# A state-space layer, a quantised feed-forward, attention and a latent layer in one kernel: where extractions, additions, broadcasts and PSUM readers stand in the scan loop

## The chip, the cores and the metric

One core of a Trainium2 chip. The kernel's work is spread over the core's engines: TensorE (PE, with weight loads as PEld) multiplies matrices into PSUM, VectorE (DVE), ScalarE (ACT) and GpSimd (POOL) work on tiles of 128 partitions, and SyncE (SP) issues most of the DMAs. Each engine runs its own queue in order and waits on semaphores for the others. The metric is the time of one execution on the device, in microseconds (us), as the median of three runs.

## The reference, cut to what matters

```python
x = x + _layernorm(_L0_attn_ref(_layernorm(x)))   # state-space layer (below)
x = x + _layernorm(_L0_ffn_ref(_layernorm(x)))    # 4-bit weights, unpacked from int32 words
x = x + _layernorm(_L1_attn_ref(_layernorm(x)))   # attention within each token
x = x + _layernorm(_L1_ffn_ref(_layernorm(x)))    # latent and shared feed-forward

# state-space layer: proj = h @ W_in.T; x, gate = halves; x = silu(conv(x))
ts, Bm, Cm = rms(ssm[..., :32]), rms(ssm[..., 32:48]), rms(ssm[..., 48:64])   # ssm = x @ W_x.T
dt = softplus(ts @ W_dt.T + b_dt)
state = state * exp(dt * A) + (dt * x) * B        # over 512 tokens, 1024 channels, 16 states
y = sum_n(state * C) + x * D;  out = (y * silu(gate)) @ W_out.T

# 4-bit weights: q = words[k // 8] >> (k % 8 * 4) & 15;  w = q * s - (z + 1) * s
```

x is 2 x 512 x 512 (batch, token, feature) in float32. The work of this case lies in the state-space layer and in the unpacking of the 4-bit weights, which runs beside it.

## The kernel before

The two batch halves (b = 0, 1) of 512 tokens are worked one after the other. A first part prepares half 0: norm, input projection, convolution, SiLU, the 64 ranks (32 for dt, 16 for B, 16 for C), their norm (`ranks_norm`, line 476) and their transposition (`ranks_out`, line 507), which writes the B and C rows to DRAM (`scr`) and loads them back broadcast to all 128 partitions (`states`, line 515): eight pairs of 512 KB tiles B and C, one pair for every two states.

**The scan loop** (line 1021) then takes 128 steps: 2 halves x 8 channel tiles x 8 pairs of states (`gi`). Of a step s:

- `exps` (ScalarE) makes the decays exp(dt x A) into one of two PSUM buffers,
- `times_B` (VectorE, L976) multiplies dt x u, which lies in PSUM, by the broadcast B into a `bx` tile, one of six,
- `scan` (VectorE, L980) runs the recurrence over 1024 elements, in place,
- `times_C` (GpSimd, L986) multiplies by C, in place,
- `sums` (TensorE, L999) adds the two states into the PSUM tile `y`; at the start of a channel tile a diagonal matmul adds x x D. `fin` (VectorE, L1005) multiplies y into the gate two steps into the next channel tile.

All other work is fitted around these by hand. `stream()` (line 919) is a generator of TensorE work in a fixed order: gate projections of half 0, transposed norms and x projections of half 1, its ranks and gates, the output projection of half 0, and the first tiles of its feed-forward. In each step it is drawn on until a budget of 3.5 us is used. Its results go to two shared PSUM banks, handed out in turn: a tile may take a bank when the one before the last has been released. Whoever reads a bank is a *job*, started with `spawn(generator, lag)`: `tick()` counts half steps in `now[0]` and runs each job that is due; a job's `yield n` puts its next part n half steps on. A step calls `tick()` (odd count, right behind the last scan), then `times_B(s + 1)`, `tick()` (even count), then `scan(s)`, `exps(s + 2)` and `times_C(s)`. `pin()` fixes the order of TensorE, ScalarE, VectorE and GpSimd as traced; SyncE's order is left to the scheduler, which keeps to priorities.

Jobs that this case speaks of: `gate_job` (three ScalarE instructions, and two half steps later a GpSimd product, L652), `x_job` (ScalarE, three convolution instructions on VectorE, L457, ScalarE, a GpSimd product, L703), `dt_job` (softplus on ScalarE between two table loads), `out_job` with `add_normed` and `norm_one` (layer norm and addition to x, L819), `ffn_up_job` (the product of gate and up, L898), and `words_job`. The last starts `gw.steps()` every four half steps: an extraction of four bits of each word on VectorE (`nibble`, L224), a conversion on ScalarE, two GpSimd products with zeros and scales (L278, L279) and a GpSimd DMA to DRAM. It begins with `gw.move` (line 253), which loads the remaining words, scales and zeros into other tiles, since those of the first part are given up; the first of them is needed by the extraction behind scan 3 (counted from 0).

After the loop TensorE finishes the feed-forward tiles that the stream has left, then runs the output projection of half 1 (L1080) and the down projection of half 0 (L1102), while VectorE and GpSimd unpack the down weights (`once`, line 291). The rest of the model follows and is not touched.

Of the kernel before, what the change touches and what calls it, by code (L numbers as in the profile page):

```python
# [18 lines left out]
P = 128  # L19
# [10 lines left out]
N_ST = 16  # L30
# [26 lines left out]
def tile_sandwich(  # L57
# [96 lines left out]
    def xs(b):  # L154
        return x[b * TB : (b + 1) * TB]
# [17 lines left out]
    def normed_T(b, dst, bank, xnew, name, **kw):  # L173
        norm_tiles(b, range(TB), dst, bank, xnew, name, **kw)

    wgu_d = dram.tile([P, 2, KH, INTER], F32, tag="wgu", name="wgu_d")
# [47 lines left out]
    class GateUpWords:  # L226
# [39 lines left out]
        def steps(self, eng=nc.gpsimd):  # L266
            n0, n1, qw, z, s, q_, w_, j = self.todo.pop(0)
            n, nm = n1 - n0, f"gu{n0}_{j}"
            q = q_(nm)
            nibble(q[:, :n], qw[:, :n], j)  # L270
            yield 2
            w = w_(nm)
            if eng is nc.vector:
                eng.tensor_sub(w[:, :n], q[:, :n], z[:, :n])
            else:
                nc.scalar.copy(w[:, :n], q[:, :n])
                yield 2
                eng.tensor_sub(w[:, :n], w[:, :n], z[:, :n])  # L278
            nc.gpsimd.tensor_mul(w[:, :n], w[:, :n], s[:, :n])  # L279
            hp_ = KH * RG  # L280
            rows = slice(j % 2 * hp_, (j % 2 + 1) * hp_)
            nc.gpsimd.dma_start(
                out=wgu_d[rows, :, j // 2, n0:n1].rearrange("r a n -> (r a) n"), in_=w[:, :n]
            )
            yield 2
# [118 lines left out]
    with ExitStack() as mamba:  # L404
# [71 lines left out]
        def ranks_norm(b, ps):  # L476

            sq = jrow(f"sq{b}")[:, : TB * N_ROW].rearrange("p (i r n) -> p i r n", i=TB, n=N_ST)
            nc.scalar.activation(sq.rearrange("p i r n -> p i (r n)"), ps, AF.Square)
            yield 2  # L480
            ss = stat.tile([P, TB, N_ROW // N_ST], F32, tag="ss", name=f"ss{b}")
            nc.vector.tensor_reduce(ss, sq, AX.X, ALU.add)

            nc.vector.tensor_add(ss[:, :, 1], ss[:, :, 0], ss[:, :, 1])
            nc.vector.tensor_scalar(ss[:, :, 1], ss[:, :, 1], 0.5, None, ALU.mult)
            r = stat.tile([P, TB, 3], F32, tag="rr", name=f"rr{b}")
            nc.vector.tensor_scalar(r, ss[:, :, 1:], 1.0 / N_ST, 1e-6, ALU.mult, ALU.add)
            yield 1
            nc.gpsimd.tensor_tensor(r, r, mhalf3, ALU.pow)
            yield 3  # L490
            nb = jrow(f"nb{b}")[:, : TB * N_ROW].rearrange("p (i r) -> p i r", i=TB)
            nc.vector.tensor_mul(
                nb[:, :, :R_DT], ps[:, :, :R_DT], r[:, :, 0:1].to_broadcast([P, TB, R_DT])
            )
            nc.vector.tensor_mul(
                nb[:, :, R_DT:].rearrange("p i (r n) -> p i r n", n=N_ST),
                ps[:, :, R_DT:].rearrange("p i (r n) -> p i r n", n=N_ST),
                r[:, :, 1:3].unsqueeze(3).to_broadcast([P, TB, 2, N_ST]),
            )
            st["nb", b] = nb  # L500
# [116 lines left out]
        with ExitStack() as p2:  # L617
# [11 lines left out]
                das.append(da)  # L629


            jobs, now = [], [0]

            def spawn(gen, lag=0):
                jobs.append([now[0] + lag, gen])
# [48 lines left out]
            def gate(b, c):  # L684
                w = w_in(1, b, c)
                if c + 2 - c % 2 < NCH:
                    w_in(1, b, c + 2 - c % 2)
                ps = yield from bank(f"pg{b}_{c}")
                yield from in_proj(b, ps, w, c % 2)
                spawn(gate_job(b, c, ps), 3)  # L690

            def x_job(c, ps):
                uc = u[1][c] = new_u(f"u1_{c}")
# [12 lines left out]
            def proj_x(c):  # L706
                w = w_in(0, 1, c)
                if c + 2 - c % 2 < NCH:
                    w_in(0, 1, c + 2 - c % 2)
                while now[0] < 2 * (NGI * (c - 3) + 4):  # L710
                    yield None
                ps = yield from bank(f"px1_{c}")
                yield from in_proj(1, ps, w, c % 2)
                spawn(x_job(c, ps), 3)

            def until(key, lag):
                while st.get(key, 1 << 30) + lag > now[0]:
# [23 lines left out]
            def turned(name, dst):  # L741

                for i in range(TB):
                    yield from until((name, i), 2)
                    tp = yield from bank(f"tp_{name}_{i}")
                    tp = tp.rearrange("p (k t) -> p k t", k=KH)
                    for kc in range(KH):
                        nc.tensor.transpose(tp[:, kc, :], st[name, i, "xn"][:, ts(kc, P)], ident)

                    def out(i=i, tp=tp):  # L750
                        nc.scalar.copy(dst[:, :, ts(i, P)], tp)
                        release(f"tp_{name}_{i}")
                        st[name, i, "free"] = st[name, "out"] = now[0]
                        yield 1

                    spawn(out(), 3)
                    yield MM / 2
                for i in range(TB):
                    while (name, i, "free") not in st:
                        yield None  # L760
# [9 lines left out]
            def ranks1():  # L770
                yield from until(("u1", NCH - 1), 3)
                pm = yield from bank("psm1")
                pm = pm[:, : TB * N_ROW].rearrange("p (i r) -> p i r", i=TB)
                for i in range(TB):
                    for c in range(NCH):
                        ranks_of(1, c, i, pm)
                        if c % 4 == 3:
                            yield MM
                spawn(ranks1_job(pm), 3)

            def rows1():
                yield from until("nb1", 1)
                pt = yield from bank("pt1")
                ranks_rows(1, pt)

                def out():
                    ranks_out(1, pt)
                    release("pt1")
                    st["rows1"] = now[0]
                    yield 1  # L790

                spawn(out(), 3)
                yield MM / 2

            def norm_one(b, i, name):
# [13 lines left out]
            def add_normed(b, i, src, o):  # L809

                name = f"mo{b}_{i}"
                mv = moments([src], name)
                yield 1
                rs = rstd(mv, name, 1)
                nm = minus_mean(mv, rs, name, 1, True)
                yield 4
                apply(o, src, rs, nm, 0)
                yield 3
                nc.vector.tensor_add(xs(b)[i], xs(b)[i], o)  # L819

            w_out = W_outT.rearrange("(j k p) h -> j p k h", p=P, k=2)

# [18 lines left out]
            def fc1_expert():  # L841

                fT = w4(fc1_wT.rearrange("p k (a n) -> p (k a) n", n=PW), "wf1T")
                fT = fT.rearrange("p (k a) n -> p k (a n)", k=LAT // P)
                ex = w4(expert_w, "wex", LAT // P, LAT)
                for a in range(KH // 2):
                    ps = yield from bank(f"pfe{a}")
                    for e in range(2):
                        for k in range(LAT // P):
                            nc.tensor.matmul(  # L850
                                ps[:, ts(e, LAT)], fT[:, k, ts(2 * a + e, P)], ex[:, k, :],
                                start=(k == 0), stop=(k == LAT // P - 1),
                            )
                        yield MM

                    def out(a=a, ps=ps):
                        t_ = trow(f"fe{a}")
                        nc.scalar.copy(t_, ps)
                        release(f"pfe{a}")
                        nc.sync.dma_start(  # L860
                            out=wfe_d[:, 2 * a : 2 * a + 2, :].rearrange("p k n -> p (k n)"), in_=t_
                        )
                        yield 1

                    spawn(out(), 3)

            def out_tiles():
                yield from until("fin7", 0)
# [2 lines left out]
                for n, (i, j) in enumerate(todo):  # L871
# [10 lines left out]
                        )  # L882
                        yield MM
                    if j == NCH // 2 - 1:
                        spawn(out_job(i, ps), 3)

            its = {}

# [12 lines left out]
            def ffn0():  # L901
# [3 lines left out]
                for i, m in enumerate(IC):  # L905
                    j, e = divmod(i, 2)
                    for a, job in enumerate((ffn_gate_job, ffn_up_job)):
                        ps = yield from bank(f"f{'gu'[a]}0_{i}")
                        for kc in range(KH):
# [2 lines left out]
                                start=(kc == 0), stop=(kc == KH - 1),  # L912
                            )
                            yield MM
                        spawn(job(i, ps), 3)
                    if not e and j + 1 < NP:
                        wt[j + 1] = gu_weights(0, j + 1)

# [21 lines left out]
                yield from ffn0()  # L940

            def words_job():
                gw.move(g1_tile, zds)
                for _ in range(len(gw.todo)):
                    yield 4
                    spawn(gw.steps())
                yield 6
                st["words"] = now[0]
# [72 lines left out]
            for s in range(NS + 3):  # L1021
# [6 lines left out]
                for part in ((1, 0) if gi == 2 else (0, 1)):  # L1028
# [3 lines left out]
                    else:  # L1032
                        while free > 0 and s < NS:
                            if dt_due and bank_free():
                                turns.append([f"pv{dt_due}", None])
                                spawn(dt_job(dt_due, dt_in(*order[dt_due])), 3)
                                free -= MM
                                dt_due = None
                            cost = next(pe, None)
# [3 lines left out]
                tick()  # L1043
                if gi == 4 and k + 1 < len(order):
                    diag(k + 1)
                if s + 1 < NS:
                    times_B(s + 1)
                    if gi == NGI - 2 and k + 1 < len(order):
                        new_du(k + 1)
                tick()  # L1050
                if s < NS:
                    scan(s)
                    if s + 2 < NS:
                        exps(s + 2)
                    times_C(s)
# [328 lines left out]
```

## Time and profile before

| | us |
|---|---|
| median of 3 runs (lowest, highest) | 998.22 (997.73, 998.55) |
| profiled execution | 995.69 |
| its span, first to last instruction | 993.8 |
| busy TensorE | 876.3 (88%) |
| busy VectorE | 701.7 (71%) |
| busy GpSimd | 468.6 (47%) |
| busy ScalarE | 424.9 (43%) |
| first scan starts, last scan ends | 77.26, 598.90 |

In a group's line stand the source line, the engine, the operation, out<-in with shapes and count; then busy us and the mean ns of one; then the engine's idle time just before them and what ended it. In a timeline line the first number is the start, the second the duration, both in us; in brackets stands the idle time of the engine before it. Shares of busy time are averages over stages: VectorE is busy at nine tenths and more from slice 3 to slice 23 of 40, TensorE nearly all the time after that.

### The profile page before, as it was taken

To read this page: it belongs to the slowest core of one execution; us is meant where nothing else is said; L and a number is where in the kernel's file an instruction comes from. 1 tells how busy PE (TensorE), PEld (TensorE's weight loads), DVE (VectorE), ACT (ScalarE), POOL (GpSimd) and SP (SyncE) were. 2 spreads that over 40 slices of the span, in tenths; PEclk is the share of its full clock that TensorE was granted. 3 is DMA by queue.
4 is the path that set the end of the run, shared out by engine and by line. 5 is a ranking of instruction groups with operands and counts; after the bars stand their busy time and mean duration, and the time that the engine had idled before them with its cause. 6 is when DMAs were issued, how large, how long until landed. Compare 5 with 4: busy or idle time off the path is not lost.

```text
span 993.8 us, 7230 instructions
## 1 busy us (share of the span) xinstructions
PE 876.3 (88%) x2216; PEld 393.3 (40%) x2216; DVE 701.7 (71%) x785; ACT 424.9 (43%) x639; POOL 468.6 (47%) x341
## 2 busy tenths in 40 slices
PE   6966867787797999867999999999999998999994
PEld 3532323233253444323344344344544444455442
DVE  3839999999999999999999996551540005715225
ACT  4336465466565675456655641031430003322212
POOL 4546888786686776566776675420000000001002
PEclk9977988989999999999999999999999999999998
DMA  6358110100000574320011003542522131100101
GB/s 194 110 183 348 44 53 15 44 36 28 22 22 21 201 241 163 109 62 0 1 42 43 21 21 91 165 154 78 185 76 64 50 103 62 64 1 32 53 0 42
DMA packets 43608, 80.61 MB, mean 81 GB/s; under 512 B 7822, under 2 KB 20217, under 8 KB 43570
## 3 DMA queue, kind: packets, MB, share of 16 engines
q1 hardware_dynamic: 40786, 72.72, 22.4%
q0 software_dynamic: 2496, 6.92, 1.8%
q10 hardware_dynamic: 288, 0.52, 0.1%
q8 instruction: 17, 0.28, 0.1%
q14 instruction: 21, 0.17, 0.1%
HBM read 68.90 MB, written 11.24 MB: 81 GB/s over the span
## 4 chain that ended last, share of the span: by engine, by line
PE 45%; DVE 29%; issue 12%; POOL 4%; ACT 3%; DMA 1%; SPq 0%; DVEq 0%; POOLq 0%; ACTq 0%
DVE bx L980 8%; DVE bx L976 8%; PE py L999 7%; PE pd L1312 6%; PE pup L1249 5%; PE fo L1102 4%; PE fu L349 3%; PE fo L1165 3%; PE fg L349 3%; PE po L1080 3%; DVE q_gu L224 3%; POOL bx L986 2%; PE fu L910 2%; PE fg L910 2%; DVE u L457 2%
## 5 line engine op out<-in xcount | busy, mean ns | idle before, releaser
L986 POOL TENSOR_TENSOR bx<-bx,C 128x1024 f32<-128x1024 f32 x128 | 302.3, 2364 | 150.4 <-DVE bx L980 141.2
L999 PE MATMUL py<-bx,ident 128*128 128x512 f32 x512 | 254.6, 628 | 52.9 <-POOL bx L986 52.7
L980 DVE TENSOR_TENSOR_SCAN bx<-da,bx 128x1024 f32<-128x1024 f32 x128 | 291.2, 2276 | 0.8 <-ACT da L960 0.8
L960 ACT ACTIVATE da<-dt,A 128x511 f32<-128x511 f32 x256 | 176.7, 691 | 206.7 <-DVE bx L980 199.6
L999 PEld LDWEIGHTS py<-bx,ident 128*128 128x128 f32 x512 | 98.2, 199 | 191.9 <-issue 104.4
L976 DVE TENSOR_TENSOR bx<-du,B 128x1024 f32<-128x1024 f32 x128 | 154.3, 1206 | 10.0 <-DMA B<-scr 7.8
L1178 DVE TENSOR_TENSOR it<-it,fu 128x512 f32<-128x512 f32 (+1 forms) x11 | 7.6, 687 | 72.3 <-PE fu L349 72.3
L1249 PE MATMUL pup<-hT_l,wup 128*128 128x512 f32 x128 | 57.6, 605 | 0.0
L674 PE MATMUL pg<-xT,w_g 128*128 128x512 f32 x120 | 56.6, 605 | 0.0
L363 POOL TENSOR_TENSOR sd<-ve,half 128x4 f16<-128x4 f16 x2 | 2.1, 1044 | 114.3 <-DVE ve L361 114.3
L1312 PE MATMUL pd<-wdn,hid 128*128 128x512 f32 x128 | 55.3, 592 | 0.0
L457 DVE SCALAR_TENSOR_TENSOR u<-px,ch,u 128x511 f32<-128x511 f32 (+2 forms) x48 | 35.7, 744 | 14.7 <-ACT u L450 13.3
L910 PE MATMUL fu<-hT_f,wu 128*128 128x512 f32 (+1 forms) x88 | 40.8, 593 | 1.0 <-DVE it L898 1.0
L127 POOL TENSOR_TENSOR rs_lo<-ve_lo,mhalf 128x1 f32<-128x1 f32 x8 | 5.5, 683 | 76.7 <-DVE ve_lo L125 76.7
L349 PE MATMUL fg<-hT_f,wg 128*128 128x512 f32 (+1 forms) x88 | 40.2, 593 | 0.7 <-ACT hT_f L171 0.7
L910 PE MATMUL fg<-hT_f,wg 128*128 128x512 f32 (+1 forms) x88 | 40.5, 592 | 0.0
L349 PE MATMUL fu<-hT_f,wu 128*128 128x512 f32 (+1 forms) x88 | 39.8, 593 | 0.0
L1165 PE MATMUL fo<-wd,it 128*128 128x512 f32 (+1 forms) x88 | 39.6, 592 | 0.0
L1102 PE MATMUL fo<-wd,it 128*128 128x512 f32 (+1 forms) x88 | 37.9, 592 | 0.0
L1312 PEld LDWEIGHTS pd<-wdn,hid 128*128 128x128 f32 x128 | 24.2, 190 | 30.7 <-issue 30.1
L674 PEld LDWEIGHTS pg<-xT,w_g 128*128 128x128 f32 x120 | 23.5, 197 | 31.1 <-issue 30.1
L1249 PEld LDWEIGHTS pup<-hT_l,wup 128*128 128x128 f32 x128 | 24.2, 192 | 28.7 <-issue 28.7
(224 smaller groups left out, 1156.2 us busy)
## 6 DMA issues: line engine op xcount, KB each, us to landing
wo<-in_W_outT SPq DMA_DIRECT2D x20, 512.0 KB
B<-scr SPq DMA_DIRECT2D x16, 512.0 KB
C<-scr SPq DMA_DIRECT2D x16, 512.0 KB
wg<-wgu_d SPq DMA_DIRECT2D x10, 512.0 KB
wu<-wgu_d SPq DMA_DIRECT2D x10, 512.0 KB
w_x<-in_W_in SPq DMA_DIRECT2D x8, 512.0 KB
wgu_d<-w_gu POOLq DMA_DIRECT2D x16, 256.0 KB, 2.4
w_g<-in_W_in SPq DMA_DIRECT2D x8, 512.0 KB
```

Source lines behind the costliest of these rows:

```text
L349: nc.tensor.matmul(ps[:m], w[:, kc, e * P : e * P + m], hT[:, kc, :], start=(kc == 0), stop=(kc == KH - 1),)
L674: nc.tensor.matmul(ps, w[:, k, ts(e, P)], xT[b][:, k, :], start=(k == 0), stop=(k == KH - 1))
L910: nc.tensor.matmul(ps[:m], wt[j][a][:, kc, e * P : e * P + m], hT[:, kc, :], start=(kc == 0), stop=(kc == KH - 1),)
L960: nc.scalar.activation(das[s % 2][:, i, 1:], st["dt", b, c][:, 1:], AF.Exp, scale=A[:, c, n : n + 1])
L976: nc.vector.tensor_mul(bx, st["du"].unsqueeze(1).to_broadcast([P, NG, S]), Bbs[b][gi])
L980: nc.vector.tensor_tensor_scan(flat, das[s % 2].rearrange("p n t -> p (n t)"), flat, 0.0, ALU.mult, ALU.add)
L986: nc.gpsimd.tensor_mul(bxs[s], bxs[s], Cbs[b][s % NGI])
L999: nc.tensor.matmul(st["y"], ident, bx[:, i, :], start=False, stop=(n == N_ST - 1))
L1102: nc.tensor.matmul(fo[t], its[i][:m, ts(t, P)], w[:m, e], start=(i == 0), stop=(i == len(IC) - 1),)
L1165: nc.tensor.matmul(fo[t], its[i][:m, ts(t, P)], w[:m], start=(i == 0), stop=(i == len(IC) - 1),)
L1249: nc.tensor.matmul(ps, w[:, kc, ts(e, P)], src[kc], start=(kc == 0), stop=(kc == KH - 1))
L1312: nc.tensor.matmul(pd, hid[kc][:, ts(i, P)], wdn[kc], start=(kc == 0), stop=(kc == INT // P - 1),)
```

## The change

Seven edits. (1) An extraction waits, a half step at a time, until `now` is odd (`scans` is filled when the loop's part begins). (2) The rank norm's mean squares: two reductions, one over 32 columns and one over 2 x 16, in place of one over 4 x 16 with an addition and a halving; two small instructions, not one, add the epsilon. (3) For half 1 the two products with the norm go from VectorE to GpSimd. (4) The additions of `add_normed` to x go from VectorE to GpSimd, issued one half step sooner. (5) The loads of `gw.move` are issued behind the last B and C broadcast of half 0. (6) In step 0 `times_B(1)` follows `scan(0)`. (7) Readers of the shared banks are spawned with a lag of 2, not 3, in nine places.

```diff
@@ steps @@
             q = q_(nm)
+
+            while scans and now[0] % 2 == 0:
+                yield 1
             nibble(q[:, :n], qw[:, :n], j)
@@ ranks_norm @@
-            ss = stat.tile([P, TB, N_ROW // N_ST], F32, tag="ss", name=f"ss{b}")
-            nc.vector.tensor_reduce(ss, sq, AX.X, ALU.add)
-
-            nc.vector.tensor_add(ss[:, :, 1], ss[:, :, 0], ss[:, :, 1])
-            nc.vector.tensor_scalar(ss[:, :, 1], ss[:, :, 1], 0.5, None, ALU.mult)
+            ss = stat.tile([P, TB, 3], F32, tag="ss", name=f"ss{b}")
+            nc.vector.tensor_reduce(
+                ss[:, :, 0], sq[:, :, : R_DT // N_ST].rearrange("p i r n -> p i (r n)"), AX.X, ALU.add
+            )
+            nc.vector.tensor_reduce(ss[:, :, 1:], sq[:, :, R_DT // N_ST :], AX.X, ALU.add)
             r = stat.tile([P, TB, 3], F32, tag="rr", name=f"rr{b}")
-            nc.vector.tensor_scalar(r, ss[:, :, 1:], 1.0 / N_ST, 1e-6, ALU.mult, ALU.add)
+            nc.vector.tensor_scalar(r[:, :, 0], ss[:, :, 0], 1.0 / R_DT, 1e-6, ALU.mult, ALU.add)
+            nc.vector.tensor_scalar(r[:, :, 1:], ss[:, :, 1:], 1.0 / N_ST, 1e-6, ALU.mult, ALU.add)
...
-            nc.vector.tensor_mul(
+            eng = nc.gpsimd if b else nc.vector
+            eng.tensor_mul(
                 nb[:, :, :R_DT], ps[:, :, :R_DT], r[:, :, 0:1].to_broadcast([P, TB, R_DT])
             )
-            nc.vector.tensor_mul(
+            eng.tensor_mul(
                 nb[:, :, R_DT:].rearrange("p i (r n) -> p i r n", n=N_ST),
...
@@ gate, and likewise proj_x, turned, ranks1, rows1, fc1_expert, out_tiles, ffn0 and dt_job @@
-                spawn(gate_job(b, c, ps), 3)
+                spawn(gate_job(b, c, ps), 2)
@@ add_normed @@
-                yield 3
-                nc.vector.tensor_add(xs(b)[i], xs(b)[i], o)
+                yield 2
+                nc.gpsimd.tensor_add(xs(b)[i], xs(b)[i], o)
+                yield 1
@@ words_job @@
-                gw.move(g1_tile, zds)
+                with tc.issue_after(last.ins):
+                    gw.move(g1_tile, zds)
@@ the loop @@
-                if s + 1 < NS:
+                if 0 < s < NS - 1:
                     times_B(s + 1)
...
                 if s < NS:
                     scan(s)
+                    if s == 0:
+                        times_B(1)
```

More of the change, by code (lines that the diff above doesn't have):

```diff
@@ L174, in normed_T @@
         norm_tiles(b, range(TB), dst, bank, xnew, name, **kw)
+    scans, now = [], [0]
     wgu_d = dram.tile([P, 2, KH, INTER], F32, tag="wgu", name="wgu_d")
@@ L629, in tile_sandwich @@
                 das.append(da)
-            jobs, now = [], [0]
+            jobs = []
+            scans.append(1)
             def spawn(gen, lag=0):
@@ L713, in proj_x @@
                 yield from in_proj(1, ps, w, c % 2)
-                spawn(x_job(c, ps), 3)
+                spawn(x_job(c, ps), 2)
             def until(key, lag):
@@ L754, in out @@
                         yield 1
-                    spawn(out(), 3)
+                    spawn(out(), 2)
                     yield MM / 2
@@ L778, in ranks1 @@
                             yield MM
-                spawn(ranks1_job(pm), 3)
+                spawn(ranks1_job(pm), 2)
             def rows1():
@@ L790, in out @@
                     yield 1
-                spawn(out(), 3)
+                spawn(out(), 2)
                 yield MM / 2
@@ L863, in out @@
                         yield 1
-                    spawn(out(), 3)
+                    spawn(out(), 2)
             def out_tiles():
@@ L884, in out_tiles @@
                     if j == NCH // 2 - 1:
-                        spawn(out_job(i, ps), 3)
+                        spawn(out_job(i, ps), 2)
             its = {}
@@ L914, in ffn0 @@
                             yield MM
-                        spawn(job(i, ps), 3)
+                        spawn(job(i, ps), 2)
                     if not e and j + 1 < NP:
@@ L1035, in tile_sandwich @@
                                 turns.append([f"pv{dt_due}", None])
-                                spawn(dt_job(dt_due, dt_in(*order[dt_due])), 3)
+                                spawn(dt_job(dt_due, dt_in(*order[dt_due])), 2)
                                 free -= MM
```

## The prediction

> **What bounds the kernel now.** I read the chain of waits first, then the groups of the page, then the timeline engine by engine through the scan loop, and last the busy times by stretch.
>
> ```profile
> PE 45%; DVE 29%; issue 12%; POOL 4%; ACT 3%; DMA 1%; SPq 0%; DVEq 0%; POOLq 0%; ACTq 0%
> ...
> L986 POOL TENSOR_TENSOR bx<-bx,C 128x1024 f32<-128x1024 f32 x128 | 302.3, 2364 | 150.4 <-DVE bx L980 141.2
> L999 PE MATMUL py<-bx,ident 128*128 128x512 f32 x512 | 254.6, 628 | 52.9 <-POOL bx L986 52.7
> L980 DVE TENSOR_TENSOR_SCAN bx<-da,bx 128x1024 f32<-128x1024 f32 x128 | 291.2, 2276 | 0.8 <-ACT da L960 0.8
> ```
>
> The scan loop runs from 77.26 to 598.90 us, 128 steps. VectorE (DVE) is idle 0.8 us before all its scans together, while GpSimd (POOL) waits 141.2 us for them: VectorE sets the pace. An undisturbed step is 3.31 us from scan to scan (394.19 to 397.50 below), one product with B (1.20) and one scan (2.28), each starting 0.08 before the last ends. 128 such steps are 424 of the loop's 522 us; the rest is what else stands in VectorE's queue, so an instruction taken from it there is worth its duration. After the loop the bound changes:
>
> ```profile
> 484.00:604.00 120.00, 116.09 (x264) 49.77 (x263) 112.78 (x77) 65.67 (x100) 86.29 (x41) 0.99 0.12 33
> 604.00:655.00 51.00, 49.15 (x115) 20.91 (x114) 27.68 (x49) 6.56 (x12) 20.68 (x19) 1.00 0.48 158
> ```
>
> After stretch and length, the columns are busy TensorE, weight load, VectorE, ScalarE, GpSimd. From 604 to 655 TensorE works 49 of 51 us: there a matmul less is time less.
>
> **1. Extractions behind a scan.** `now` is odd in the half step behind a scan. The word job starts at 4, waits 4 more, and its spawned steps first run one half step later, at 9, 13, 17: every extraction of the loop is already at an odd half step. In the built program none moves. What they cost:
>
> ```profile
> 109.52 0.42 DVE L224 TENSOR_SCALAR q_gu<-qw_gu 128x512 int32<-128x512 int32 x1
> ...
> 117.07 7.30 DVE L224 TENSOR_SCALAR q_gu<-qw_gu 128x512 int32<-128x512 int32 x1
> 117.11 1.28 POOL L652 TENSOR_TENSOR g<-th,g 128x512 f32<-128x512 f32 x1
> ...
> 118.34 4.64 POOL L986 TENSOR_TENSOR bx<-bx,C 128x1024 f32<-128x1024 f32 x2
> ...
> 122.94 1.15 POOL L278 TENSOR_TENSOR w_gu<-w_gu,zs_gu 128x512 f32<-128x512 f32 x1
> ```
>
> Alone an extraction takes 0.31 to 0.42; at 117.07 it lasted until GpSimd's queue first broke, after g, two bx and the first w_gu. The thirteen in the loop take 27.2 us (timeline), 22.5 over 13 x 0.36. [...] The row shows four, and an extraction that already stood behind the scan. I take the row: 0 from the move. GpSimd's silu products (L652, L703, 1.27) do shift by a half step (part 5) and so change what an extraction meets; GpSimd is busy 108.7 of the 142 us from 73 to 215 and falls behind at every second word, with the same work after. I take **+1**, from -4 (one more 4 us wait) to +7 (the waits at 175.76 and 199.07, 3.7 + 1.9, go behind convolutions that now come earlier, and some more).
>
> **2. B's broadcast first, and the moved word loads.**
>
> ```profile
> 63.24 0.33 SPq L511 DMA_DIRECT2D scr<-bc  x1
> 63.68 0.59 SPq L218 DMA_DIRECT2D zs_gu<-in_gate_s  x1
> ...
> 66.09 0.40 SPq L520 DMA_DIRECT2D B<-scr  x1
> ...
> 73.74 1.23 DVE L976 TENSOR_TENSOR bx<-du,B 128x1024 f32<-128x1024 f32 x1 [6.67 <-DMA B<-scr]
> ...
> 76.12 1.23 DVE L976 TENSOR_TENSOR bx<-du,B 128x1024 f32<-128x1024 f32 x1 [1.15 <-DMA B<-scr]
> ...
> 77.26 2.28 DVE L980 TENSOR_TENSOR_SCAN bx<-da,bx 128x1024 f32<-128x1024 f32 x1
> ...
> 89.40 0.94 DVE L224 TENSOR_SCALAR q_gu<-qw_gu 128x512 int32<-128x512 int32 x1
> ```
>
> Four loads of scales and zeros stand ahead of B on SyncE and in its DMA queue; the slowest ends at 72.4 (SyncE's wait at 72.44). Without them B can be issued when scr has landed (64.85, its semaphore) and land some 2.9 later (66.09 to 69.0, as on the DMA engines that the four did not hold up): 67.8. The first scan waits for its decays (ScalarE, 67.66 + 1.4): 69.1 instead of 77.26, and it no longer stands behind the second product. The 16 broadcasts land 1.24 apart (SyncE issues 73.64, 74.89, 76.11), so B of step 4 lands near 78 and VectorE reaches the extraction behind scan 3 (counted from 0) at about 83.5, not 89.4: 6 us ahead.
>
> But this extraction reads the words whose loads were moved. On SyncE two qw loads now stand behind all 16 broadcasts and four x tiles. C7 lands at 67.8 + 15 x 1.24 = 86.4 (to 87.7, if the queue starts as slowly as in the trace, C0 2.5 after B0), four x at 0.65 make 89.0, two qw at 0.65 (landings 60.57 and 61.24) 90.3 to 91.6. VectorE waits 7 us there, and products, scans and GpSimd wait behind it. The extraction then takes 0.4, not 0.94: ends 91.3 against 90.34. The lead is used up: **-1**, from -2.2 to +1.
>
> **3. The second half's rank norm and its products.**
>
> ```profile
> 300.65 0.69 DVE L1005 TENSOR_TENSOR g<-g,py 128x512 f32<-128x512 f32 x1 [2.11 <-PE py L999]
> ...
> 305.01 2.20 DVE L484 TENSOR_TENSOR ss<-ss 128x4 f32<-128x4 f32 x1
> ...
> 314.18 0.67 DVE L492 TENSOR_TENSOR nb<-pr,rr 128x128 f32<-128x128 f32 x1
> 314.76 2.42 DVE L495 TENSOR_TENSOR nb<-pr,rr 128x128 f32<-128x128 f32 x1
> ```
>
> ss, ss, ss, rr lengthen their step by 2.97 (6.28 - 3.31); two reductions (0.3 each, under the 0.40 of the whole) and two 0.17 cost 0.95: +2.0. They now stand three steps earlier, ahead of the 2.11 wait for py, which shrinks by their 0.95: +0.9. nb leaves VectorE: +3.0. On GpSimd it is about 0.5 each, behind a 2.30 power; then TensorE transposes, and bc (0.68) now stands between a product with B and its scan: it waits about 1: net +2.0. The first half's norm gains and loses two small instructions ahead of the 2.4 power: 0. **Sum +5**, 3 to 6.
>
> **4. Additions to x.**
>
> ```profile
> 397.50 2.28 DVE L980 TENSOR_TENSOR_SCAN bx<-da,bx 128x1024 f32<-128x1024 f32 x1
> 399.70 1.20 DVE L976 TENSOR_TENSOR bx<-du,B 128x1024 f32<-128x1024 f32 x1
> 400.81 2.02 DVE L819 TENSOR_TENSOR x<-x,o 128x512 f32<-128x512 f32 x1
> ```
>
> The four in the loop take 2.02, 2.01, 2.01 and 0.67: 6.7. On GpSimd they are 1.27 each (L652, same shape, both inputs in SBUF). [...] three of four waited out a product with C (399.92 to 402.28), and GpSimd is idle 0.95 a step here, so 6.7 go. Behind x2 and x3 the statistics of x follow within a step and may wait 0.5: **+6.2**, 5 to 6.7. The other four come after the loop: done by 667, 20 us before TensorE's next transposes; nothing.
>
> **5. Readers two half steps behind, not three.** A bank is freed half a step earlier, so TensorE's stream moves ahead. Counted in the built program, six matmuls of 128x512 (0.86 each) more are issued before the last sums: 5.2 us less after 604, where TensorE is the bound: **+5**, 3 to 5.2 (a late output weight could hide some; its load now stands earlier on SyncE).
>
> The price is in the loop. An up projection's product on VectorE (L898) and ScalarE's readers come half a step earlier, in order, with scans or decays behind them. Where a tile's last matmul and its release fall in one step (four of the eight L898 in the loop), sums start after C ends (2.5 after the scan), two passes of 1.72 later the tile is done: 5.9 + TensorE's lag behind the scan two steps back, against VectorE arriving at 3.5 + 1.2 + its extras: 0.6 + lag. The lag (start of sums less end of C) is 0.05 to 4.9, in the last 40 steps mostly 0.4 to 3. Four waits of 0.6 + 1 to 1.5 are 7, less 2.4 for waits at L898 and bx already there (0.49, 0.47, 0.46, 0.48, 0.5), less what each catches up for the next. One L898 more in the loop adds 0.66, and a softplus between two table loads can delay the decays where the lag is over 1.8. **-4**, from -11 to 0.
>
> **Sum:** +1 - 1 + 5 + 6.2 + 5 - 4 = 12. The profiled execution took 995.69 (span 993.8 and 1.9 around it) and would take 983.5; it is 2.5 under the runs' median of 998.22, so I predict **986**.
>
> **Rivals.** (a) Earlier readers cost more than all else gains: TensorE, busy 116 of 120 us before 604, is awaited by some 46 readers in the loop (15 gates, 8 x, 15 dt, 8 up). At 0.5 each they cost 23 us against the 16 of the other parts: 1005. It decides from 0.35 per reader on; against it, in TensorE's order most readers follow a step after their last matmul. 7%. (b) The extractions find GpSimd idle, as the silu products now spread between the words: up to 22, 967. For: six of thirteen already take under 0.42. Against: GpSimd's queue is as long. 10%. (c) The lead of part 2 survives: the words arrive before 85 and 5 us stay, 980. Against: SyncE's order. 10%. (d) VectorE's freed time goes into waits for TensorE; only the end is won: 994. For: the 2.11 wait and lags up to 4.9. Against: from 360 to 484 TensorE is busy 105 of 124. 15%. My forecast has 58%, own range 980 to 991.
>
> **Range** 975 to 995, which takes in (c), (d) and half of (b). A change within 0.2% (2 us) can't be told from none. Faster 0.87, same 0.06, slower 0.07.
>
> **What would show it.** Scan 0 near 69, a wait of some 7 us for qw ahead of scan 4, which starts again at 91 to 93; several extractions of 2 to 7 us; no L484, nb and x on GpSimd and steps of 3.31 there; waits for fu or ScalarE between a product and its scan after 480; six matmuls fewer after the loop. I am wrong if scan 4 starts before 89, or if the waits of the last 40 steps pass 12 us.

## The result and the profile after

The changed kernel takes **990.93 us** (990.79 to 991.52, four runs) against 997.98 (996.54 to 998.55, four runs) of the kernel before on the same chip: a ratio of 0.9939, 95% interval 0.9920 to 0.9958. So 7 us are gained where 12 were forecast (986, range 975 to 995). The profiled execution took 991.02, span 989.0. Against before's profiled 995.69 that is 4.7, not 7: before's profiled execution lay 2.3 under this median (2.5 under the one of three runs above), this one on its own. The sums below are between these two traces.

From the page after, the shares of the chain of waits and three rows of the costliest groups:

```profile
PE 39%; DVE 31%; issue 12%; POOL 7%; ACT 2%; DMA 2%; SPq 1%; DVEq 0%; POOLq 0%; ACTq 0%
...
L996 POOL TENSOR_TENSOR bx<-bx,C 128x1024 f32<-128x1024 f32 x128 | 301.9, 2360 | 142.2 <-DVE bx L990 131.0
L1009 PE MATMUL py<-bx,ident 128*128 128x512 f32 x512 | 257.2, 633 | 57.6 <-POOL bx L996 57.4
L990 DVE TENSOR_TENSOR_SCAN bx<-da,bx 128x1024 f32<-128x1024 f32 x128 | 291.4, 2277 | 0.1
```

The regime is unchanged: VectorE is idle ahead of its scans 0.1 us in all, GpSimd waits 131.0 us for them. The chain runs less over TensorE than before (45%) and more over GpSimd (4%). What changed is what VectorE waits for between the scans. Its eight longest waits in the loop of the changed kernel (total us, times, longest):

```profile
DVE q_gu L226 <- DMA qw_gu<-in_up_q: 7.1, 1, 7.1
DVE it L907 <- PE fu L919: 5.8, 4, 2.5
DVE bx L986 <- DMA B<-scr: 3.4, 2, 3.0
DVE bc L516 <- PE pt L511: 2.2, 1, 2.2
DVE bx L986 <- issue: 1.2, 1, 1.2
DVE du L984 <- ACT du L978: 0.9, 1, 0.9
DVE st_mo L119 <- ACT o L840: 0.7, 1, 0.7
DVE st_f L119 <- POOL x L827: 0.4, 1, 0.4
```

Of these eight kinds only the waits for B (7.8 us) and for du (0.4) stood in the kernel before. The other six are new, 17.4 us together, and the first two make up most of it. The waits for y (2.1), for `it` on GpSimd (1.4), for the decays (0.8) and of a product with B for TensorE (0.5) are gone, and what stood on VectorE for the rank norm and for x is less; so is what remains after the loop.

The first of them, in VectorE's timeline (start, duration, in brackets the wait):

```profile
69.64 1.22 DVE L986 TENSOR_TENSOR bx<-du,B 128x1024 f32<-128x1024 f32 x1 [2.95 <-DMA B<-scr]
70.97 2.29 DVE L990 TENSOR_TENSOR_SCAN bx<-da,bx 128x1024 f32<-128x1024 f32 x1
...
82.60 2.28 DVE L990 TENSOR_TENSOR_SCAN bx<-da,bx 128x1024 f32<-128x1024 f32 x1
91.97 0.43 DVE L226 TENSOR_SCALAR q_gu<-qw_gu 128x512 int32<-128x512 int32 x1 [7.09 <-DMA qw_gu<-in_up_q]
92.31 1.22 DVE L986 TENSOR_TENSOR bx<-du,B 128x1024 f32<-128x1024 f32 x1
93.45 2.28 DVE L990 TENSOR_TENSOR_SCAN bx<-da,bx 128x1024 f32<-128x1024 f32 x1
```

The first scan starts at 70.97 instead of 77.26. Scan 3 ends at 84.88, and the extraction behind it stands 7.09 us for its words: scan 4 starts at 93.45, where it was 91.4 before. The lead of 6.3 has become a loss of 2.1.

The word stage, in the timeline of the changed kernel:

```profile
119.15 7.32 DVE L226 TENSOR_SCALAR q_gu<-qw_gu 128x512 int32<-128x512 int32 x1
119.19 2.35 POOL L996 TENSOR_TENSOR bx<-bx,C 128x1024 f32<-128x1024 f32 x1
...
121.49 1.28 POOL L660 TENSOR_TENSOR g<-th,g 128x512 f32<-128x512 f32 x1
...
122.72 2.34 POOL L996 TENSOR_TENSOR bx<-bx,C 128x1024 f32<-128x1024 f32 x1
125.03 1.14 POOL L283 TENSOR_TENSOR w_gu<-w_gu,zs_gu 128x512 f32<-128x512 f32 x1
```

This is the extraction that lasted 7.30 before, again until GpSimd had worked off four instructions, though it is recorded 0.04 us ahead of the first of them. The thirteen of the loop take 28.0 us (27.2 before).

### The profile page after: what moved, and what is told of

It is laid out like the page before. It is cut to its first block, busy times and chain, and to the rows that moved or that the text cites. A ratio compares the mean times of both kernels' runs of the same rounds, so it can differ in the third digit from the quotient of the medians.

```text
span 989.0 us, 7214 instructions
## 1 busy us (share of the span) xinstructions
PE 878.8 (89%) x2216; PEld 393.8 (40%) x2216; DVE 688.8 (70%) x775; ACT 426.0 (43%) x639; POOL 478.3 (48%) x351
## 4 chain that ended last, share of the span: by engine, by line
PE 39%; DVE 31%; issue 12%; POOL 7%; ACT 2%; DMA 2%; SPq 1%; DVEq 0%; POOLq 0%; ACTq 0%
DVE bx L990 11%; DVE bx L986 8%; PE py L1009 6%; PE pup L1261 5%; POOL bx L996 4%; PE fo L1114 4%; PE pd L1324 4%; PE fu L354 3%; PE fo L1177 3%; PE fg L354 3%; DVE q_gu L226 3%; PE fu L919 2%; PE fg L919 2%; DVE u L462 1%; PE pr L1292 1%
## 5 line engine op out<-in xcount | busy, mean ns | idle before, releaser
L996 POOL TENSOR_TENSOR bx<-bx,C 128x1024 f32<-128x1024 f32 x128 | 301.9, 2360 | 142.2 <-DVE bx L990 131.0
L1009 PE MATMUL py<-bx,ident 128*128 128x512 f32 x512 | 257.2, 633 | 57.6 <-POOL bx L996 57.4
L1009 PEld LDWEIGHTS py<-bx,ident 128*128 128x128 f32 x512 | 98.5, 200 | 195.1 <-issue 97.2
L226 DVE TENSOR_SCALAR q_gu<-qw_gu 128x512 int32<-128x512 int32 (+1 forms) x24 | 34.3, 1428 | 7.1 <-DMA qw_gu<-in_up_q 7.1
```

The lines of the kernel that those rows point to most:

```text
L226: nc.vector.tensor_scalar(q, qw, 4 * j, 15, ALU.logical_shift_right, ALU.bitwise_and)
L996: nc.gpsimd.tensor_mul(bxs[s], bxs[s], Cbs[b][s % NGI])
L1009: nc.tensor.matmul(st["y"], ident, bx[:, i, :], start=False, stop=(n == N_ST - 1))
```

## The experiments

Each edit is made on the changed kernel unless said otherwise; lines and names are its own. The stretches come from the starts of the scans in the profiled executions (steps counted from 0), in us:

| kernel | scan 0 | scan 4 | steps 4-41 | 41-54 | 54-88 | 88-126 | last scan ends | rest | clock in the rest | median |
|---|---|---|---|---|---|---|---|---|---|---|
| before | 77.3 | 91.4 | 177.0 | 53.2 | 134.3 | 138.6 | 598.9 | 394.9 | 0.98 | 997.98 |
| changed | 71.0 | 93.4 | 177.3 | 49.6 | 130.6 | 142.9 | 598.2 | 390.8 | 0.97 | 990.93 |
| lag 3 everywhere | 71.5 | 94.2 | 177.0 | 50.6 | 128.8 | 138.3 | 593.3 | 396.5 | 0.97 | 990.51 |
| x on VectorE | 70.5 | 93.8 | 177.3 | 49.6 | 133.6 | 143.3 | 602.1 | 390.8 | 0.97 | 994.10 |
| old rank norm | 71.8 | 94.9 | 177.3 | 53.5 | 130.6 | 142.9 | 603.6 | 390.7 | 0.97 | 994.01 |
| old order of loads | 78.2 | 92.1 | 177.3 | 49.6 | 130.5 | 142.9 | 596.8 | 390.8 | 0.97 | 988.55 |
| up readers at 3 | 71.5 | 94.1 | 177.3 | 49.6 | 132.2 | 137.6 | 595.2 | 390.4 | 0.97 | 984.10 |
| words ahead | 71.0 | 87.2 | 177.3 | 49.6 | 130.3 | 144.7 | 593.6 | 391.3 | 0.97 | 985.19 |
| words every 5 | 71.4 | 86.9 | 174.5 | 53.0 | 128.8 | 143.5 | 591.2 | 392.3 | 0.96 | 983.39 |
| strided extraction | 70.8 | 94.8 | 167.5 | 50.0 | 130.3 | 142.9 | 590.0 | 390.4 | 0.97 | 982.37 |
| three edits | 71.5 | 87.5 | 168.7 | 50.0 | 130.5 | 137.2 | 578.3 | 387.5 | 0.98 | 967.79 |
| three, gapped | 72.0 | 87.7 | 165.5 | 49.6 | 130.3 | 137.1 | 574.8 | 392.8 | 0.96 | 968.42 |
| three, two more at 3 | 70.4 | 87.4 | 167.6 | 47.8 | 132.6 | 137.2 | 577.1 | 388.7 | 0.97 | 969.02 |

Scan 0 moves by up to 1.6 us between kernels that start alike, and the medians of before by 1.8 between the five sets of runs (997.61 to 999.42), so single microseconds are read from the stretches and not from the medians. The clock is the mean that TensorE was granted behind the last scan, where it is the bound. The kernels with lag 2 leave the same TensorE work there (992 or 993 records), and its time goes with the clock: 387.5 at 0.98, 388.7 to 391.3 at 0.97, 392.3 and 392.8 at 0.96. So two rests are set against each other at one clock.

### One part undone at a time

**Readers at lag 3 again.**

```diff
-                spawn(gate_job(b, c, ps), 2)
+                spawn(gate_job(b, c, ps), 3)
...
```

> All nine readers stand three half steps behind again; the other parts of the change stay. Theory A (lag 2 wins the end and gives it back in the loop): the stretch after the last scan grows from 390.75 back to some 395, the loop's end comes 4 to 5 earlier (593 to 595), the waits for fu at the last 40 steps go, the time is 990 to 992, as in the changed kernel. Rival B (lag 2 is also what makes bc wait 2.23 at step 54 and what puts the waits of 0.69 and 0.91 for ScalarE at step 70): the loop gains a further 3, and the time is 987. Rival C (lag 2 carries the gain): 995 or more.

Measured: 990.51, ratio to before 0.9926 (0.9905 to 0.9947), the same as the changed kernel. The loop is 4.9 shorter and the rest 5.7 longer. Theory A: lag 2 gives back in the loop what it wins at the end. Behind the last scan the trace has 1004 TensorE records where the changed kernel's has 992; a matmul of 512 columns leaves two (L1009: 512 records for 128 steps of two matmuls), so six more are left. Two waits in VectorE's list of this kernel show that the loop's waits trade places:

```profile
DVE g L1015 <- PE py L1009: 2.8, 1, 2.8
DVE it L907 <- POOL it L660: 1.4, 3, 0.5
```

The waits for fu, for pt and for ScalarE's copy of po are gone; y is waited for again, as before the change (2.1).

**The additions to x on VectorE again.**

```diff
-                yield 2
-                nc.gpsimd.tensor_add(xs(b)[i], xs(b)[i], o)
-                yield 1
+                yield 3
+                nc.vector.tensor_add(xs(b)[i], xs(b)[i], o)
```

> The four additions to x of the loop (and the four after it) are on VectorE again; the rest is as in the changed kernel. Theory A (the prediction's term): they cost 6.2 there, 997. Theory A' (the term is as the stretch of steps 70 to 88 showed it, part of the freed time going into waits for GpSimd's x and for ScalarE): 3.7, 994.5. Rival (all of the freed time goes into waits): 991.

Measured: 994.10, ratio 0.9953 (0.9936 to 0.9969); steps 54 to 88 take 3.0 more, the loop ends 3.9 later. Theory A', but not for its reason. VectorE's timeline in this kernel:

```profile
395.34 2.28 DVE L989 TENSOR_TENSOR_SCAN bx<-da,bx 128x1024 f32<-128x1024 f32 x1
397.54 0.66 DVE L827 TENSOR_TENSOR x<-x,o 128x512 f32<-128x512 f32 x1
398.12 1.22 DVE L985 TENSOR_TENSOR bx<-du,B 128x1024 f32<-128x1024 f32 x1
```

Before the change this addition stood behind the product with B, at 400.81, in the middle of GpSimd's product with C, and took 2.02. With lag 2 it comes at the other half step, straight behind the scan, and takes 0.66; GpSimd's product with C, recorded from 397.76, takes 2.66 there and not 2.36. Three of the four take 0.66 to 0.67 here, one 2.01: 4.0 in all, not 6.7. Part 5 alone had removed most of the collisions that part 4 was to remove.

**The old rank norm** (one reduction, addition and halving, one epsilon instruction; `eng = nc.vector`).

> The rank norm as it was before: one reduction, the addition and the halving on VectorE, both products nb on VectorE. Theory A (the prediction's term): 5 slower than the changed kernel, 996. Theory A' (steps 41 to 54 as traced): 3.6, 994.5. Rival (the wait of 2.23 for the row transposes stays whatever stands ahead of it, and later waits take the rest): under 1.5, 991 to 992.5.

Measured: 994.01, ratio 0.9959 (0.9940 to 0.9979). Steps 41 to 54 take 3.9 more; the further 1.5 of its later loop end stand ahead of step 4, which the edit doesn't touch. Theory A'. The old form, in this kernel's timeline:

```profile
296.73 0.41 DVE L487 TENSOR_REDUCE ss<-sq 128x16 f32<-128x256 f32 x1
297.18 1.08 DVE L488 TENSOR_TENSOR ss<-ss 128x4 f32<-128x4 f32 x1
298.29 0.17 DVE L489 TENSOR_SCALAR ss<-ss 128x4 f32<-128x4 f32 x1
298.50 0.17 DVE L491 TENSOR_SCALAR rr<-ss 128x12 f32<-128x12 f32 x1
```

and the new form, in the changed kernel's:

```profile
295.33 0.28 DVE L487 TENSOR_REDUCE ss<-sq 128x4 f32<-128x128 f32 x1
295.53 0.27 DVE L490 TENSOR_REDUCE ss<-sq 128x8 f32<-128x128 f32 x1
295.72 1.14 DVE L492 TENSOR_SCALAR rr<-ss 128x4 f32<-128x4 f32 x1
296.77 0.16 DVE L493 TENSOR_SCALAR rr<-ss 128x8 f32<-128x8 f32 x1
```

1.83 against 1.85: the collision has passed from the removed addition to the first of the new instructions. GpSimd's product with C runs from 294.47 to 296.83 beside it. What the part is worth is nb, 1.23 + 2.43 in this kernel. The wait of 2.2 for pt is there in both, and not at lag 3: it is part 5's. So is the end of the wait for y: neither has it, and the new form at lag 3 waits 2.8.

**The old order of loads** (`gw.move` without `issue_after`, `times_B(1)` ahead of `scan(0)`).

> Words' loads no longer held behind the broadcasts, and the second product with B ahead of the first scan again: part 2 undone alone. Theory A (the lead of 6.3 us is lost in the 7.1 us wait for qw): the first scan at 77.3 instead of 71.0, no wait for qw, step 4 at 91 instead of 93.4, the time 1 to 2 us shorter, 989 to 990. Rival (the lead of the first scan is worth what it shows and something later eats it): 995 or more.

Measured: 988.55, ratio 0.9902 (0.9880 to 0.9924). Scan 0 at 78.2, no wait for qw, scan 4 1.4 earlier than in the changed kernel; the loop ends as much earlier, and nothing behind scan 4 differs. Theory A: part 2 as built loses a little. The ratios alone don't show it, as their intervals overlap; but scan 4 starts at 93.4 to 94.9 in the six kernels that have part 2 as built and read the words behind scan 3, and at 91.4 and 92.1 in the two without it.

### Taking away one new wait, and one old one

**Only the up readers at lag 3.** (`a` is 0 for gate, 1 for up.)

```diff
-                        spawn(job(i, ps), 2)
+                        spawn(job(i, ps), 2 + a)
```

> Only the readers of the up projections (ffn_up_job, eight in the loop) stand three half steps behind again; the other eight kinds of reader stay at two. Theory A (the four waits for fu, 5.76 us together, are the whole price of lag 2 in the loop): steps 107 to 126 take some 69.5 again instead of 74.7, at most two matmuls (1.7) come back behind the loop: 986.5 to 988. Rival (TensorE's work sets both: what VectorE gains in the loop is late again at the end): 990 to 991.5.

Measured: 984.10, ratio 0.9873 (0.9851 to 0.9896). VectorE's list of waits from 484 on:

```profile
DVE it L907 <- PE fu L919: 0.4, 1, 0.4
DVE it L907 <- POOL it L660: 0.2, 1, 0.2
```

Steps 88 to 126 take 137.6 instead of 142.9, and the rest stays at 390.4, with 992 records again. Theory A: the gain at the end doesn't hang on the readers that cost the most. The median lies below A's range. The profiled execution, 987.53, is the slowest of its six: behind scan 68 a product with B waits 2.8 us where the changed kernel's waited 1.2 (the row "issue" above). The clock differs too. The same 8 us in the changed kernel, at lag 3 everywhere, and here (busy times as in the prediction's stretches; behind GpSimd's stands the granted clock):

```profile
363.00:371.00 8.00, 7.67 (x14) 3.36 (x15) 8.00 (x6) 5.34 (x8) 5.48 (x3) 0.79 0.58 206
363.00:371.00 8.00, 8.00 (x23) 4.26 (x24) 8.00 (x6) 6.44 (x8) 6.10 (x4) 1.00 0.46 164
363.00:371.00 8.00, 6.67 (x9) 2.90 (x10) 8.00 (x6) 4.81 (x8) 5.47 (x3) 0.57 0.54 189
```

At 1.00 there is no such wait. Of the thirteen traces, three show no drop of the clock just ahead of this product (before, lag 3 everywhere, words every five half steps, which has lag 2), and only these three have no wait there; the other ten wait 0.9 to 1.3, and 2.8 here. So the wait goes with the clock, and not with the lag alone. Whether the readers' places bring on the drop, which ten of the eleven kernels with lag 2 have, is open.

**The words ahead of the fifth pair of broadcasts.** The two qw loads go behind the first four pairs, then the other eight broadcasts and x, then scales and zeros (`move` calls `rest` between the qw loads and these).

```diff
-            for gi in range(NGI):
+            for gi in range(4):
                 last = states(0, gi)
...
+            def rest(got):
+                with tc.issue_after(got.ins):
+                    for gi in range(4, NGI):
+                        states(0, gi)
+                    load_x(1)
+            with tc.issue_after(last.ins):
+                gw.move(g1_tile, zds, rest)
```

> B first, as in the changed kernel, but the two qw loads of the moved words stand behind the fourth pair of broadcasts, ahead of the other eight broadcasts and of x; scales and zeros stay at the end. Theory A (the lead of the first scan was lost only in the wait for qw): no wait at the extraction behind scan 3, step 4 at 86 to 87.5 instead of 93.4, nothing later takes it back: 984 to 985.5. Rival B (the extraction then meets the products with C on GpSimd[...], or B of step 5 to 7 is late): step 8 gains 2 to 4, 987 to 989. Rival C (the lead is worth nothing): 991.

Measured: 985.19, ratio 0.9873 (0.9849 to 0.9897). Its timeline, where the changed kernel stood for 7.09 us:

```profile
83.23 2.28 DVE L988 TENSOR_TENSOR_SCAN bx<-da,bx 128x1024 f32<-128x1024 f32 x1
85.43 0.72 DVE L228 TENSOR_SCALAR q_gu<-qw_gu 128x512 int32<-128x512 int32 x1
86.07 1.21 DVE L984 TENSOR_TENSOR bx<-du,B 128x1024 f32<-128x1024 f32 x1
87.20 2.27 DVE L988 TENSOR_TENSOR_SCAN bx<-da,bx 128x1024 f32<-128x1024 f32 x1
```

Scan 4 starts 6.2 earlier than in the changed kernel, scan 88 is still 6.5 ahead, and the loop ends 4.6 earlier, after another 1.8 of waits for fu. Theory A: the lead was lost in this one wait.

**Words every five half steps** (`yield 4` to `yield 5` in `words_job`).

> The words are spawned every five half steps instead of every four; all else as in the changed kernel. Theory A (an extraction waits because GpSimd still works off the word before, the g product and the products with C): the thirteen extractions of the loop, 28 us with the changed kernel, take 18 to 22, and steps 4 to 54 are 6 to 10 us shorter: 981 to 985. Rival B (each waits for the product with C of its own step, whatever the distance): 28 again, 990 to 992. Rival C (later words put gate products and the rank norm of the second half late): over 993.

Measured: 983.39, ratio 0.9845 (0.9819 to 0.9871). Theory A, and some of C. Scan 41 starts at 261.4 instead of 270.7: 3.3 of this come from the wait for qw (3.8 instead of 7.1, as the first extraction comes a step later), and most of the rest from the thirteen extractions, which take 20.3 instead of 28.0. The distance between words does set what an extraction meets. Then the later rank norm gives back 3.4 in steps 41 to 54: bc waits 5.0 for pt instead of 2.2.

**An extraction read at a stride.** That another form of it would not wait beside GpSimd was the author's estimate, which no run before this one shows. In the loop 511 elements are read as 73 x 7 (351 as 27 x 13), at a stride of 73 (27) elements, and the last one by itself:

```diff
-            nibble(q[:, :n], qw[:, :n], j)
+            m, a = n - 1, 7 if n == S else 13
...
+                nibble(q[:, :m], qw[:, :m].rearrange("p (a b) -> p b a", a=a), j)
+                nibble(q[:, m:n], qw[:, m:n], j)
...
```

> The loop's extractions[...]: 511 (or 351) elements read as 73 x 7 (27 x 13) and written flat, in another order that ScalarE's copy puts right, and the last element by itself. Theory A[...]: each takes 0.6 and 0.1, none waits, thirteen take 9 to 10 instead of 28: 972 to 975. Rival B (GpSimd, behind by then, becomes the bound of these steps: sums and buffers of bx wait for it): half, 980 to 983. Rival C ([...]strided reads cost as much): 990 or more.

Measured: 982.37, ratio 0.9839 (0.9813 to 0.9865). The extraction that took 7.32, now in two pieces, in this kernel's timeline, and three of VectorE's waits in its loop:

```profile
119.76 0.66 DVE L1027 TENSOR_TENSOR g<-g,py 128x512 f32<-128x512 f32 x1
120.33 1.15 DVE L226 TENSOR_SCALAR q_gu<-qw_gu 128x511 int32<-128x511 int32 x2
121.40 1.21 DVE L998 TENSOR_TENSOR bx<-du,B 128x1024 f32<-128x1024 f32 x1
```

```profile
DVE du L996 <- ACT du L990: 3.2, 2, 2.3
DVE u L474 <- ACT u L467: 2.4, 2, 2.0
DVE g L1027 <- PE py L1021: 1.7, 1, 1.7
```

The thirteen take 13.7 instead of 28.0, and none waits, as in theory A; as the two pieces of each overlap by up to 0.1, 12.6 of VectorE's time. Of the 15.4 saved the steps 4 to 41 keep 9.8; the rest went into new waits, for du at step 14 (2.3), y at step 17 (1.7) and u at step 18 (2.0). ScalarE's copies of the thirteen take 12.4 and 2.8 us here, the changed kernel's 6.7, and may have a part in that, which is not shown (the gapped form below has short copies, and waits for du for longer). The size falls into B's range, but B's reason, that GpSimd becomes the bound, could show only in the wait for y. And the strided read costs more than A's 0.6 (1.04 to 1.08 for 511).

### A version that beats both

**The three edits together** (words ahead, up readers at 3, strided extraction).

> Three edits together on the changed kernel: qw loads ahead of the fifth pair of broadcasts, the readers of the up projections at three half steps, and the extractions in the strided form of 73 x 7 (27 x 13). Theory A (the three prices are paid at different places and add): 5.8 + 6.9 + 8.6 off the changed kernel's 991, 970. Rival B (with the words on time[...] VectorE arrives early everywhere, and the waits that the strided form had for TensorE and ScalarE between steps 14 and 18, 6.0 together, grow by most of the lead): 975 to 977.

Measured: **967.79**, ratio to before 0.9692 (0.9676 to 0.9707), 23 us under the changed kernel. Theory A: the loop ends 19.9 earlier, of the 21.3 that its three prices (5.8, 6.9, 8.6) add up to, although rival B's waits are there (VectorE now waits 3.9 for du at step 14 and 3.5 for u at step 18). The other 3.3 lie behind the loop, where none of the edits acts and TensorE was granted 0.98 of its clock and not 0.97.

**The extraction read in order and written with a gap** (7 rows of 73 into rows of 74, 13 of 27 into rows of 28; ScalarE's copy closes the gaps). In the built program the source is one run of 511 elements (351), the destination 7 rows of 73 (13 of 27).

> As the run with the three edits, but the extraction reads its words in order and writes them with a gap (7 x 73 of rows of 74, and 13 x 27 of rows of 28). Theory A ([...]the strided read alone was what made 511 elements take 0.81 to 1.08): 0.55 to 0.6 for 511 and 0.4 for 351, no waits; thirteen are 5 us shorter, and 2 to 5 of that stay. Rival B (waits for TensorE and ScalarE take it): the same time as the run before. Rival C[...]: extractions of 2 to 7 us again, and 6 to 9 more than the run before.

Measured: 968.42, ratio 0.9698 (0.9685 to 0.9712): the same time as the three edits. 511 elements take 0.66 to 0.68, 351 take 0.49 to 0.51, no waits: A for the read in order, though it takes longer than A's 0.55 to 0.6 and 0.4. ScalarE's copies take 6.7 and 2.4. The loop ends 3.6 us earlier in the profiled execution, but the wait for du grows to 5.3, and what follows the loop is 5.4 longer. Two rows of busy times by stretch after the loop, of the three edits and then of this kernel; the column behind GpSimd's is the granted TensorE clock:

```profile
650.00:700.00 50.00, 46.60 (x155) 23.33 (x154) 22.48 (x54) 17.48 (x24) 2.77 (x3) 1.00 0.39 126
700.00:750.00 50.00, 47.89 (x124) 21.56 (x123) 8.47 (x19) 9.51 (x17) 1.30 (x2) 1.00 0.24 68
```

```profile
650.00:700.00 50.00, 48.06 (x151) 24.12 (x150) 23.19 (x56) 18.36 (x28) 3.07 (x3) 0.93 0.38 126
700.00:750.00 50.00, 47.89 (x121) 21.89 (x120) 7.84 (x18) 8.44 (x15) 1.01 (x1) 0.97 0.24 68
```

TensorE was granted 0.93 and 0.97 where the other execution had 1.00. It is not this one execution alone: the mean clock of the whole span is 0.959 to 0.966 in its four, and 0.966 to 0.970 in the five of the three edits. Whether the shorter loop brings it on is open, and so is what the 3.6 are worth.

**Two more kinds of reader at 3** (rows1's `out` and `out_job`, on top of the three edits).

> As the run with the three edits, with two more kinds of reader at three half steps: that of the row transposes (rows1) and that of the output tiles (out_job). Theory A (two half steps are too few for any reader on VectorE whose tile TensorE ends in the same step: bc's wait of 2.23 for pt at step 51 and the wait of 0.70 for ScalarE's copy of po at step 70 come from it, and no matmul goes back behind the loop): 2 to 3.5 shorter, 964 to 966. Rival (the waits only change place: bc goes behind the product with B of a later step, the statistics meet the softplus and du all the same): 967 to 968.5, as that run.

Measured: 969.02, ratio 0.9705 (0.9678 to 0.9732). The rival: bc no longer waits and steps 41 to 54 gain 2.2, but du then waits 1.2 for ScalarE at step 54, and two additions more are waited for on GpSimd (1.6 us in three waits): steps 54 to 88 lose 2.1.

## Why the prediction was right, and where its sizes were off

The time fell into the range, on the forecast's side of no change; 5 us of the forecast 12 are missing by the medians (7.3 by the traces). By its own steps, forecast against the traces of before and after, whose differences add up to the 4.7:

- **Extractions, +1:** -0.3 (steps 4 to 41). Nothing moved, as said: without the two lines of the new wait the built program is the same, instruction for instruction. The row with its four GpSimd instructions was the right one to go by.
- **B first, -1:** -2.1. The place and the size of the wait were right (7 for qw ahead of scan 4, measured 7.09; the words read at 91.97, forecast 90.3 to 91.6). Scan 0 came at 71.0, not 69.1, since the first B, issued at 64.53, took 5.1 to reach its reader (69.64) and not 2.9. Undoing the part alone gains 1.4 at scan 4 and words ahead gains 6.2, so that the reason is shown from both sides.
- **Rank norm, +5:** +3.6 (3.9 undone alone), in the new schedule all of it the products nb. The other terms were mis-sized, and it is luck that their errors partly cancel. "ss +2.0" was worth nothing: 2.94 became 1.85, but at lag 2 the old form takes 1.83, since the new epsilon instruction meets GpSimd as the addition does. The wait for y that was to shrink by 0.9 went whole (2.1), and bc waited 2.2, not 1; both came with lag 2 and not with the new norm.
- **x, +6.2:** +3.7 over steps 54 to 88, the term that was furthest off. Its 6.7 was read in the old schedule, in which three additions collide, while part 5 moves them to where they cost 4.0 in all; undoing the part costs 3.0. And the stretch holds a term that the sum put at nothing: the drop of the clock at 363, which goes with the wait of 1.2 behind scan 68. Where it is missing, steps 54 to 88 take 128.8 and not 130.6: at lag 3 everywhere, which is the schedule in which x was priced (5.4 off the 134.3 of before), and with lag 2 in words every five.
- **Lag 2, +5 at the end and -4 in the loop:** +4.1 and -4.3 (steps 88 to 126), and +5.7 and -4.9 with the part undone alone. The 5.7 compares two executions at a clock of 0.97 in the rest; the 4.1 sets one at 0.97 against before's at 0.98. Both mechanisms, six matmuls and four waits for fu, are as forecast.

Of the rivals, earlier readers costing more than all else (a) and idle GpSimd (b) did not come; the lead (c) did not survive but could have, as words ahead shows; and freed VectorE time that goes into other waits (d) holds in part: the waits for pt, po and du are such.

## What to carry to other kernels

Price the parts of a change in the schedule that the other parts make: a collision that one part removes may be gone already by another, as x's was. When a load is put behind a queue of others, look for the first instruction that reads it: one word load ate the whole lead, and moving two DMAs gave 6 us. Before a stretch is set against a forecast, look at the clock that it was granted: here a short drop goes with waits of 0.9 to 2.8 us, where the parts of the change are worth 2 to 5. And a reader that stands in order on the bounding engine wants its operand early, not itself early: delaying one kind of reader by a half step gave 5 us in its stretch and cost nothing at the end.

## What the runs showed of the hardware

- A VectorE extraction recorded 0.04 us ahead of GpSimd's next instruction (119.15 and 119.19) lasted 7.32 us, through four GpSimd instructions in a row. In two other forms, with GpSimd as busy in the loop (383.9 and 383.8 us from 70 to the last scan's end, against 384.7), the same extraction takes 1.08 and 0.68. What in the form makes the difference is not shown.
- Read in order and written with a gap, 511 int32 elements take 0.66 to 0.68; read at a stride of 73 elements, 1.04 to 1.08. The old form took 0.42 for 512 where GpSimd stood idle as it started (109.52 in the kernel before).
- A small instruction was held up as well: one of 4 elements per partition took 1.14 in the changed kernel, ending with GpSimd's product with C (296.86 and 296.83), and 2.27 with lag 3, where the one of 8 that follows it takes 0.16.
- Behind the loop the time goes with the clock that TensorE was granted (387.5 at 0.98 to 392.8 at 0.96 for the same instructions). In the loop a drop to a mean of 0.79 over 8 us goes with a wait of 1.2 on VectorE, and one to 0.57 with 2.8.
